# A graph network's setup in written order: first edges found eight at a time, one-hots from 16 bit operands, layer norm on ACT and POOL

## The chip, the cores and the metric

One core of a Trainium2 chip. The time is device time in microseconds, the median of several executions. Engines are named as in the profile: PE (matrix multiplications), DVE (vector operations), ACT (activations), POOL (which also issues the indirect transfers, that is gathers and scatters), SP (which here only issues plain transfers).

## The reference, cut to what matters

6250 nodes with 64 features, 206250 edges sorted by destination dst, so that the edges of a node lie together. Layer 0 and then three attention layers:

```python
h = relu(layernorm(x))
# layer 0: messages along edges, mean over the edges of a node
msg = relu(concat(h[dst], edge_attr_16) @ W1 + b1)
x = x + relu(segment_sum(msg, dst) / max(count, 1) + h @ Wres + bres)
h = relu(layernorm(x))
# three attention layers over the same edges, with edge_attr_32
for l in range(3):
    q, k, v, e = h @ Wq + bq, h @ Wk + bk, h @ Wv + bv, edge_attr_32 @ We
    a = softmax over the edges of a node of (q[dst] * (k[src] + e)) / sqrt(C)
    h = segment_sum(a * (v[src] + e)) + h @ Ws + bs      # and prelu after the first two
x = x + h
```

## The kernel before, in words

The nodes are padded to 6272 = 49 x 128 and sorted by their number of edges (degree). Block b holds the 128 nodes of about equal degree, one in each partition; its nodes get CAP[b] slots for edges (66 in block 0, 22 in block 48), of which LEAST[b] are surely filled.

**Setup** (gnn_kernel, lines 115 to 373, to 127 us). It finds where the edges of each node begin, counts degrees, sorts the nodes, and writes the table tabx with a row of 192 numbers for each node: -(h W1 + b1), h(W1 + Wres) + both biases, and x.
- *Coarse search.* dst is loaded twice, one shifted by one edge (prev, cur; 127 and 126), into space that belongs to k.rows. first (179) takes every 256th edge; pb (182) spreads it to all partitions through PE; count on DVE (191) or signs on ACT (196) count how many are below a node. From that run_i (204) picks, for each partition and each of 7 groups g of 7 nodes, where a window of 728 edges is gathered (got, 209).
- *Fine search.* For each of the 49 nodes of a partition and one more, a pass over the window counts the edges below it: 21 on ACT straight from the integers, 29 on DVE from a cast (look_f, 237).
- *Sort.* start, deg and the class cls come from that (249 to 269); oh (280) is a one-hot of the class, cnt, cum and at (282 to 297) give each node its place; half (304) splits it in column and row.
- *Permutation.* In seven rounds of seven nodes, one-hots to and blk and the products val = blk x of (312 to 319) are made on DVE, and PE multiplies them into pperm (321). join and what follows give at_i (first edge), num_i (number of the node), deg of each sorted node.
- *Rows of x* (334 to 370). In seven groups of seven blocks: sums, squares and root of the layer norm on DVE, POOL and ACT, transposes (361), relu to hT (364), projection with wn (367), copy to rx (368), x itself beside it (369), and write-back to tabx (370).
- src is turned (225 to 233) into edge order in DRAM (srcs).
- A check that dst does not fall (fall, 216) goes into bad; if any check fails, another path computes the result.

In this part the order of each engine's instructions is chosen by a scheduler that may interleave the sections above.

**Layer 0** (layer0, 443) is ordered by hand on POOL, PE, ACT and DVE: each engine runs its instructions as they stand in the code. For block b, POOL gathers edge attributes four blocks ahead (load_e, 457), rows of tabx (load_x, 463), src (load_src, 470) and edge_attr_32 six blocks back (load_ea). PE turns attributes (turn, 483), and messages (494) does PE products, DVE maxima and a tree of sums, 16 slots at a time; after each such chunk one entry of todo runs. finish(g) (538) closes a group of blocks (FIN0: 8, 8, 8, 8, 8, 4, 3, 2): it makes the new x, its sums, and on ACT the squares and root (562 to 565), and leaves the rest in todo: norm on DVE (568, 570), project, rows. put (594) scatters a row to the attention table, at most two in a block, LATE = 5 blocks after its group closed (626); the rest are put after the loop.

**Attention** (attention, 685), three layers: POOL gathers kv rows one slot of a block at a time (704, by way of 429), DVE does the arithmetic.

Of the kernel before, what the change touches and what calls it, by code (L numbers as in the profile page):

```python
# [25 lines left out]
F16 = mybir.dt.float16  # L26
AF = mybir.ActivationFunctionType
# [69 lines left out]
def gnn_kernel(ctx: ExitStack, tc: tile.TileContext, x, src_t, dst_t, dst_row, ea16, ea32, eaT16, eaT32, w, out):  # L97
# [17 lines left out]
    with tc.tile_pool(name="chk", bufs=1) as p, tc.tile_pool(name="chk2", bufs=2) as p2, \  # L115
            tc.tile_pool(name="n0w", bufs=2) as wp, tc.tile_pool(name="chkp", bufs=1, space=PSUM) as pp, \
            tc.tile_pool(name="n0p", bufs=2, space=PSUM) as psum:

# [6 lines left out]
        for r in (most, rest):  # L125
            nc.sync.dma_start(prev[r], by_row(dst_row[:EP])[r])
            nc.scalar.dma_start(cur[r], by_row(dst_row[1:])[r])
# [3 lines left out]
        sf = p.tile([P, T], I32, name="sf")  # L131
        nc.scalar.dma_start(sf, src_t)
        make_identity(nc, ident)
# [4 lines left out]

        nc.gpsimd.memset(k.w0blk, 0.0)
        for j in range(8):  # L140
            nc.sync.dma_start(k.w0blk[j * 16:(j + 1) * 16, j % 4 * D:(j % 4 + 1) * D], w["L0_gnn_W1"][D:, :])
        for l in range(LAYERS):
            for i, s in enumerate("qkvs"):
                nc.sync.dma_start(wl[l][:D, i * D:(i + 1) * D], w[f"L1_gnn_W{s}{l}"])
                nc.sync.dma_start(wl[l][D:D + 1, i * D:(i + 1) * D], w[f"L1_gnn_b{s}{l}"][None, :])
        nc.sync.dma_start(slope, w["L1_gnn_prelu_a"][None, :].to_broadcast([P, 1]))
        for l in range(LAYERS):
            nc.gpsimd.memset(k.wblk[l], 0.0)
            for j in range(4):
                nc.sync.dma_start(k.wblk[l][j * 32:(j + 1) * 32, j * D:(j + 1) * D], w[f"L1_gnn_We{l}"])  # L150
# [7 lines left out]

        node = iota(NB + 1, NB)
        nc.gpsimd.memset(ones, 1.0)  # L160
        iota(P, 0, f=col)
        place = iota(NB, 1, [[P, NB]])
# [4 lines left out]
        for t, values in ((k.cap, CAP), (least, LEAST)):  # L167
            for v, i, j in runs(values):
                nc.gpsimd.memset(t[:, i:j], float(v))
        going = p.tile([P, CLS, NB], BF16, name="going")  # L170
        nc.gpsimd.memset(going, 1.0)
        nc.gpsimd.memset(going[:, :, 0:1], 0.0)

        near = p.tile([P, NB + 1], F32, name="near")
        nc.vector.tensor_scalar(near, node, -0.5, None, op0=OP.add)
# [8 lines left out]
        less = p.tile([P, NB + 1], F32, name="less")  # L186
# [20 lines left out]
        for g in range(NG0):  # L207
            t = scratch[:, 2 * WE + g * LOOK:2 * WE + (g + 1) * LOOK]
            nc.gpsimd.indirect_dma_start(
                out=t, out_offset=None, in_=by_run,  # L210
                in_offset=bass.IndirectOffsetOnAxis(ap=run_i[:, g:g + 1], axis=0))
            got.append(t)

        nc.vector.memset(bad, 0.0)
        fall = p.tile([NW, WE], BF16, name="fall")
        nc.vector.tensor_tensor(fall, prev, cur, op=OP.is_gt)
        nc.vector.tensor_reduce(bad[:NW, 0:1], fall, axis=AX.X, op=OP.max)

        for t0 in range(0, T, 4 * P):
            n4 = min(4, -(-(T - t0) // P))  # L220
            ps = psum.tile([P, 4, P], F32, name="ps", tag="pr_t")
            si = wp.tile([P, 4, P], I32, name="si")
            sff = wp.tile([P, 4 * P], F32, name="sff")
            nt = min(4 * P, T - t0)
            nc.scalar.copy(sff[:, :nt], sf[:, t0:t0 + nt])
            for i in range(n4):
                n = min(P, T - t0 - i * P)
                nc.tensor.transpose(ps[:n, i, :], sff[:, i * P:i * P + n], ident)
            for i in range(n4):
                n = min(P, T - t0 - i * P)  # L230
                nc.scalar.copy(si[:n, i, :], ps[:n, i, :])
                e0 = (t0 + i * P) * P
                nc.scalar.dma_start(srcs[e0:e0 + n * P].rearrange("(t e) -> t e", e=P), si[:n, i, :])

        for g in range(NG0):
            f = p2.tile([P, LOOK], F32, name="look_f", bufs=3)
            (nc.gpsimd.tensor_copy if g else nc.scalar.copy)(f, got[g])
            for i in range(SG + (g == NG0 - 1)):
                b = SG * g + i
                if i < NA:  # L240
                    signs(got[g], b, less[:, b:b + 1], [P, LOOK], BF16)
                else:
                    count(f, b, less[:, b:b + 1], [P, LOOK], BF16)
        by_group = lambda t: t.rearrange("p (g i) -> p g i", i=SG)
        nc.vector.tensor_scalar(by_group(less[:, :NB])[:, :, :NA], by_group(less[:, :NB])[:, :, :NA], 0.5, LOOK / 2,
                                op0=OP.mult, op1=OP.add)
        start = p.tile([P, NB + 1], F32, name="start")
        nc.vector.tensor_scalar(run, run, float(RUN), -1.0, op0=OP.mult, op1=OP.add)
        nc.vector.tensor_add(by_group(start[:, :NB]), by_group(less[:, :NB]), run[:, :, None].to_broadcast([P, NG0, SG]))
        nc.vector.tensor_add(start[:, NB:], less[:, NB:], run[:, NG0 - 1:])  # L250
        nc.vector.tensor_scalar(start, start, 0.0, float(E), op0=OP.max, op1=OP.min)

        deg = p.tile([P, NB], F32, name="deg")
        nc.vector.tensor_sub(deg, start[:, 1:], start[:, :NB])
        nc.vector.tensor_scalar(deg, deg, 0.0, float(P - 1), op0=OP.max, op1=OP.min)
        whole = p.tile([P, 2, NB], I32, name="whole")
        nc.vector.tensor_copy(whole[:, 0], start[:, :NB])
# [4 lines left out]
        of = p.tile([P, NB, 4], F16, name="of")  # L262
        nc.vector.tensor_copy(of, part.rearrange("p v i b -> p b (v i)"))
        cls = p.tile([P, NB], F32, name="cls")
        nc.vector.tensor_scalar(cls, deg, float(LOW), float(HIGH[0]), op0=OP.max, op1=OP.min)
        for h in HIGH:
            nc.vector.scalar_tensor_tensor(cls, deg, float(h), cls, op0=OP.is_gt, op1=OP.add)
        nc.vector.scalar_tensor_tensor(cls, deg, 0.0, cls, op0=OP.is_gt, op1=OP.add)
        nc.vector.tensor_scalar(cls, cls, -float(LOW), float(CLS - 1), op0=OP.add, op1=OP.min)


        for l in range(LAYERS):
            nc.gpsimd.tensor_copy(k.ws[l][:, :D], wl[l][:, 3 * D:])
            nc.gpsimd.tensor_scalar(k.ws[l][:, D:2 * D], wl[l][:, :D], float(D // HEADS[l]) ** -0.5, 0.0, op0=OP.mult,
                                    op1=OP.add)
            nc.gpsimd.tensor_copy(k.ws[l][:, 2 * D:], wl[l][:, D:3 * D])


        oh = p.tile([P, CLS, NB], BF16, name="oh")
        nc.vector.tensor_tensor(oh, col[:, :CLS, None].to_broadcast([P, CLS, NB]),  # L280
                                cls[:, None, :].to_broadcast([P, CLS, NB]), op=OP.is_equal)
        cnt = p.tile([P, CLS], F32, name="cnt")
        nc.vector.tensor_reduce(cnt, oh, axis=AX.X, op=OP.add)
        pc = pp.tile([P, 2, CLS], F32, name="pc", tag="pc")
        nc.tensor.matmul(pc[:, 0, :], ones, cnt, start=True, stop=True)
        nc.tensor.matmul(pc[:, 1, :], before, cnt, start=True, stop=True)
# [7 lines left out]
        nc.vector.tensor_add(cum, cum, upto[:, :, None].to_broadcast([P, CLS, NB]))  # L294
        nc.vector.tensor_mul(cum, cum, oh)
# [7 lines left out]
        half = p.tile([P, 2, NB], F32, name="half")  # L303
        nc.vector.tensor_copy(half, half_i)
        turned = p.tile([P, NB], F32, name="turned")
# [3 lines left out]
        pperm = pp.tile([P, 4, NB], F32, name="pperm", tag="pc")  # L309
        for b0 in range(0, NB, 7):  # L310
            to = p2.tile([P, 7, P], F16, name="to")
            nc.vector.tensor_tensor(to, col[:, None, :].to_broadcast([P, 7, P]),
                                    half[:, 1, b0:b0 + 7, None].to_broadcast([P, 7, P]), op=OP.is_equal)
            blk = p2.tile([P, 7, NB], F16, name="blk")
            nc.vector.tensor_tensor(blk, col[:, None, :NB].to_broadcast([P, 7, NB]),
                                    half[:, 0, b0:b0 + 7, None].to_broadcast([P, 7, NB]), op=OP.is_equal)
            val = p2.tile([P, 7, 4, NB], F16, name="val")
            nc.vector.tensor_mul(val, blk[:, :, None, :].to_broadcast([P, 7, 4, NB]),
                                 of[:, b0:b0 + 7, :, None].to_broadcast([P, 7, 4, NB]))
# [123 lines left out]
def layer0(tc, ea16, ea32, ident, tabx, srcs, k, col, least, ones, bad, nbad_i):  # L443

    nc = tc.nc
    with tc.tile_pool(name="g0", bufs=3) as gp, tc.tile_pool(name="e0", bufs=2) as ep, \
# [152 lines left out]
        with tc.manual_schedule(engines={getattr(mybir.EngineType, e) for e in ("Pool", "PE", "Activation", "DVE")}):  # L599
# [25 lines left out]
            for b in range(NB):  # L625
# [13 lines left out]
                if b + 1 < NB:  # L639
                    turn(b + 1)  # L640
# [746 lines left out]
```

## Time and profile before

| | us |
|---|---|
| median of 8 runs (7579.67 to 7613.91) | 7593.4 |
| the profiled execution | 7585.84 |
| its span (first to last instruction) | 7584.1 |
| setup, to the first gather from tabx | 127.1 |
| layer 0, to the first gather of kv | 449.5 |
| attention | 7007.5 |

Engine totals over the span:

```profile
PE 1752.7 (23%) x4808; PEld 1105.4 (15%) x4808; DVE 3178.6 (42%) x6020; ACT 353.3 (5%) x1096; POOL 5057.7 (67%) x5212
```

How to read the lines that follow: a group's line has line, engine, operation, output<-input, shape and count, then busy time, mean ns of one, idle time just before it and what ended most of that. In the timeline the first number is the start, the second how long, and the bracket the idle time before and its releaser. In a table by stage the columns after the stage's length are busy us (and instructions) of each engine, the granted PE clock, the share of the transfer engines and GB/s. A line of waits has the total, the times and the longest.

### The profile page before, as it was taken

How to read it: one execution, taken by the hardware profiler on the slowest of the kernel's cores; microseconds unless marked ns; L12 is line 12 of the kernel's file. 1: busy time of each engine (PE TensorE's matmuls, PEld its weight loads, DVE VectorE, ACT ScalarE, POOL GpSimd, SP SyncE). 2: the span in 40 equal slices, each digit the busy share in tenths (PEclk: the TensorE clock that was granted, in tenths of full speed). 3: DMA queues.
4: the chain of work that ended last, by engine and by line, in shares of the span. 5: the costliest groups of instructions: out<-in, count | busy, mean ns of one | idle time of the engine just before them, and what ended most of it. 6: DMA issues, size and time to landing. Idle time of an engine off the chain costs nothing. (4 is left out here: it accounts for less than half of the span.)

```text
span 7584.1 us, 26893 instructions
## 1 busy us (share of the span) xinstructions
PE 1752.7 (23%) x4808; PEld 1105.4 (15%) x4808; DVE 3178.6 (42%) x6020; ACT 353.3 (5%) x1096; POOL 5057.7 (67%) x5212
## 2 busy tenths in 40 slices
PE   4652221122222222211221221222211111121111
PEld 3431111111111111100111111111111111111100
DVE  7873333353333444433443443445433333344333
ACT  2110000000000000000000000000000000000000
POOL 4566666666666665777666766765777777667775
PEclk8765555555555555555555555555555555555555
DMA  3653222222222222222222222221222222222221
GB/s 97 210 178 95 70 69 69 72 73 74 65 76 70 71 74 57 63 59 56 59 60 57 63 59 54 64 60 55 67 57 57 60 55 59 56 62 61 57 59 40
DMA packets 226262, 534.67 MB, mean 70 GB/s; under 512 B 89430, under 2 KB 105148, under 8 KB 224982
## 3 DMA queue, kind: packets, MB, share of 16 engines
q0 software_dynamic: 171200, 374.08, 19.3%
q1 hardware_dynamic: 52790, 156.27, 6.4%
q10 hardware_dynamic: 2090, 2.48, 0.1%
q14 instruction: 141, 1.16, 0.1%
q8 instruction: 41, 0.67, 0.0%
HBM read 458.63 MB, written 73.87 MB: 70 GB/s over the span
## 5 line engine op out<-in xcount | busy, mean ns | idle before, releaser
L429 POOL DMA_INDIRECT kv<-tab,src x4788 | 4697.5, 981 | 2152.4 <-issue 1549.8
L763 DVE TENSOR_TENSOR kv<-kv,pe 128x1024 f32<-128x1024 f32 (+6 forms) x663 | 737.7, 1113 | 3350.0 <-remote 2385.5
L757 PE MATMUL pe<-wblk,ea 128*128 128x256 f32 x1736 | 851.4, 644 | 2846.7 <-issue 1327.6
L757 PEld LDWEIGHTS pe<-wblk,ea 128*128 128x128 f32 x1736 | 504.5, 317 | 3166.0 <-issue 1798.3
L799 DVE TENSOR_REDUCE some<-kv 128x64 f32<-128x512 f32 (+6 forms) x690 | 611.1, 920 | 59.7 <-remote 36.4
L772 DVE TENSOR_TENSOR prod<-kv,more 128x512 f32<-128x512 f32 (+6 forms) x690 | 425.0, 627 | 152.0 <-remote 78.3
L773 DVE TENSOR_REDUCE al<-prod 128x16 f32<-128x512 f32 (+10 forms) x690 | 423.8, 626 | 104.6 <-remote 32.6
L757 PE MATMUL pe<-wblk,eaT 128*128 128x256 f32 x868 | 375.2, 588 | 300.7 <-DVE kv L763 155.7
L795 DVE TENSOR_TENSOR kv<-kv,more 128x512 f32<-128x512 f32 (+6 forms) x690 | 416.0, 625 | 0.0
L816 PE MATMUL po<-ws,ht 65*128 65x256 f32 x196 | 114.2, 686 | 1073.3 <-issue 903.9
L734 PE MATMUL turn<-ident,ea 128*128 128x128 f32 x434 | 113.8, 400 | 1013.9 <-issue 780.9
L757 PEld LDWEIGHTS pe<-wblk,eaT 128*128 128x128 f32 x868 | 249.8, 306 | 378.0 <-DVE kv L763 170.6
L734 PEld LDWEIGHTS turn<-ident,ea 128*128 128x128 f32 x434 | 70.6, 198 | 1071.8 <-issue 834.8
L816 PEld LDWEIGHTS po<-ws,ht 65*128 65x128 f32 x196 | 53.1, 313 | 1119.5 <-issue 936.2
L506 PE MATMUL pm<-w0blk,eT 64*128 64x256 f32 x868 | 177.6, 530 | 107.5 <-DVE msg L509 70.5
L429 POOL DMA_INDIRECT e<-in_ea_dram,at_i x98 | 104.5, 1067 | 127.2 <-PE turn L491 87.6
L784 ACT ACTIVATE more<-al,m 128x33 f32<-128x33 f32 (+22 forms) x245 | 72.0, 294 | 2024.4 <-issue 1058.5
L531 DVE TENSOR_TENSOR msg<-msg 128x128 f32<-128x128 f32 (+12 forms) x221 | 136.4, 617 | 7.2
L788 DVE TENSOR_REDUCE s<-more 128x2 f32<-128x66 f32 (+34 forms) x147 | 30.9, 210 | 258.5 <-ACT more L784 213.5
L506 PEld LDWEIGHTS pm<-w0blk,eT 64*128 64x128 f32 x868 | 111.5, 256 | 156.6 <-issue 76.9
L435 POOL DMA_INDIRECT out_dram<-hn,num_i x49 | 53.3, 1088 | 99.8 <-DVE hn L820 43.0
L735 ACT COPY eaT<-turn 128x512 f32<-128x512 f32 (+3 forms) x127 | 66.5, 524 | 1140.2 <-remote 813.6
(194 smaller groups left out, 1458.9 us busy)
## 6 DMA issues: line engine op xcount, KB each, us to landing
kv<-tab,src POOLq DMA_INDIRECT x4788
ea<-eat SPq DMA_DIRECT2D x26, 576.0 KB
ea<-eat SPq DMA_DIRECT2D x24, 512.0 KB
ea<-eat SPq DMA_DIRECT2D x16, 640.0 KB
ean<-e SPq DMA_DIRECT2D x13, 576.0 KB
ea<-ean SPq DMA_DIRECT2D x13, 576.0 KB
eat<-eaT SPq DMA_DIRECT2D x13, 576.0 KB
ea<-eat SPq DMA_DIRECT2D x16, 448.0 KB
```

What stands on the lines that cost most here:

```text
L429: return nc.gpsimd.indirect_dma_start(out=out, out_offset=None, in_=table, in_offset=bass.IndirectOffsetOnAxis(ap=idx, axis=0))
L506: nc.tensor.matmul(pm[:, r, u].rearrange("p j f -> p (j f)"), eT[h, t0 // 8 + u, :], k.w0blk[h, :], start=True, stop=True)
L531: nc.vector.tensor_add(msg[:, :h] if c > 2 else total, msg[:, :h], msg[:, c - h:c])
L734: nc.tensor.transpose(ps[:, i - i0, :], t[:, i, :], ident)
L757: nc.tensor.matmul(pe[:, 4 * g:4 * g + 4].rearrange("p j f -> p (j f)"), ea[:, t0 // 4 + g, :], k.wblk[l], start=True, stop=True)
L763: nc.vector.tensor_add(pair(kv[:, :m, :2 * D]), pair(kv[:, :m, :2 * D]), pe[:, :m, None, :].to_broadcast([P, m, 2, D]))
L772: nc.vector.tensor_mul(prod[:, :n], kv[:, :n, :D], q[:, None, :].to_broadcast([P, n, D]))
L773: nc.vector.tensor_reduce(al[:, :H, t0:t0 + n].rearrange("p h j -> p j h"), prod[:, :n].rearrange("p j (h c) -> p j h c", h=H), axis=AX.X, ...
L784: nc.scalar.activation(ex[:, h, :c], al[:, h, :c], AF.Exp, bias=m[:, h:h + 1])
L795: nc.vector.tensor_mul(v.rearrange("p j (h c) -> p j h c", h=H), v.rearrange("p j (h c) -> p j h c", h=H), ex[:, :H, t0:t0 + n].rearrange( ...
L799: nc.vector.tensor_reduce(some[:, i, :], v.rearrange("p j f -> p f j"), axis=AX.X, op=OP.add)
L816: nc.tensor.matmul(po, ht[:, :P], k.ws[l + 1], start=True, stop=True)
```

## The change

All of the setup now also runs in written order, on all five engines. What it does, section by section:
- SP alone issues the transfers: prev, x, the weights of layer 0, src; later the attention weights, x straight into the last third of tabx, cur, slope, We.
- Windows are cast to f32 on ACT into looks, with the group's eight nodes appended (LOOK8 = 736 elements), and one max_index per group gives the index of the first match of eight nodes. The indices are made monotone by a scan from the end. Only the last border keeps a sign pass.
- The layer norm's squares go to ACT, one block at a time between the casts; the norm itself to ACT (even quads of blocks) and POOL (odd ones).
- One-hots have the node as the innermost dimension, with col spread to 16 bit (colb); cls, half and of are 16 bit too. Two rounds (24 and 25 nodes) instead of seven. PE reads their slices [:, :, b].
- Rows of x go by quads of four blocks, q 0 to 3 before the first round's products, 4 to 6 before the second's, the rest after.
- src is turned last.
- Layer 0: the fall check comes before the first block's messages; the place column of k.rows is filled at block 3; the squares become an entry of todo, with an empty one behind; LATE is 6.

```diff
+    with tc.manual_schedule(engines={... "Pool", "PE", "Activation", "DVE", "SP"}), \
...
+        colb = [k.src[i].bitcast(F16)[:, :D * NB].rearrange("p (c b) -> p c b", b=NB) for i in range(2)]
+        nc.vector.tensor_copy(colb[0], col[:, :D, None].to_broadcast([P, D, NB]))
+        nc.scalar.copy(colb[1], col[:, D:, None].to_broadcast([P, D, NB]))
...
+        def squares(b):
+            sq = p2.tile([P, D], F32, name="sq0")
+            nc.scalar.activation(sq, xs[:, b], AF.Square, bias=negm[:, b:b + 1], accum_out=var[:, b:b + 1])
...
         for g in range(NG0):
+            nc.scalar.copy(looks[:, g, :LOOK], got[g])
+            nc.vector.max_index(place_i[:, g], node[:, SG * g:SG * g + 8], looks[:, g])
+            for b in range(2 * g, 2 * g + 2):
+                squares(b)
+        signs(got[NG0 - 1], NB, less, [P, LOOK], BF16)
+        for b in range(2 * NG0, NB):
+            squares(b)
+        nc.scalar.activation(var, var, AF.Sqrt, bias=eps[:, 0:1], scale=1.0 / D)
...
+        nc.sync.dma_start(tabx[:, 2 * D:], x)
+        for r in (most, rest):
+            nc.sync.dma_start(cur[r], by_row(dst_row[1:])[r])
...
+        nc.vector.tensor_tensor_scan(from_[:, ::-1], start[:, ::-1], start[:, ::-1], float(E), op0=OP.min, op1=OP.min)
...
+        nc.vector.reciprocal(var, var)
+        nc.vector.tensor_mul(negr, negm, var)
...
+        def norm(q):
+            for b in quads[q]:
+                if q % 2:
+                    nc.gpsimd.tensor_scalar(hn[:, b], xs[:, b], var[:, b:b + 1], negr[:, b:b + 1],
+                                            op0=OP.mult, op1=OP.add)
+                else:
+                    nc.scalar.activation(hn[:, b], xs[:, b], AF.Identity, bias=negr[:, b:b + 1], scale=var[:, b:b + 1])
...
+        def rows_of_x(q):
+            if q < len(quads):
+                norm(q)
+            if 1 <= q <= len(quads):
+                turn(q - 1)
+            if 2 <= q:
+                project(q - 2)
...
+        parts = [slice(0, 24), slice(24, NB)]
+        for i, s in enumerate(parts):
+            n = s.stop - s.start
+            for c in range(2):
+                nc.vector.tensor_tensor(to[:, c * D:(c + 1) * D, s], colb[c][:, :, s], half[:, 1:2, s].to_broadcast([P, D, n]),
+                                        op=OP.is_equal)
+            nc.vector.tensor_tensor(blk[:, :, s], colb[0][:, :NB, s], half[:, 0:1, s].to_broadcast([P, NB, n]),
+                                    op=OP.is_equal)
+            for v in range(4):
+                nc.vector.tensor_mul(val[:, v, :, s], blk[:, :, s], of[:, v:v + 1, s].to_broadcast([P, NB, n]))
+            for q in ((0, 1, 2, 3), (4, 5, 6))[i]:
+                rows_of_x(q)
+            for b in range(s.start, s.stop):
+                nc.tensor.matmul(pperm.rearrange("p v b -> p (v b)"), to[:, :, b],
+                                 val[:, :, :, b].rearrange("p v c -> p (v c)"), start=(b == 0), stop=(b == NB - 1))
...
+        for q in range(7, len(quads) + 2):
+            rows_of_x(q)
...
-            for i in range(n):
-                sq = wp.tile([P, D], F32, name="sq")
-                nc.scalar.activation(sq, x[:, i], AF.Square, bias=m[:, i:i + 1], accum_out=v[:, i:i + 1])
-            nc.scalar.activation(v[:, :n], v[:, :n], AF.Sqrt, bias=eps[:, 0:1], scale=1.0 / D)
+            def squares():
...
-            todo = [norm]
+            todo = [squares, lambda: None, norm]
...
-        AHEAD, LATE, LATER = 4, 5, 6
+        AHEAD, LATE, LATER = 4, 6, 6
...
+            nc.vector.tensor_tensor(fall, scratch[:NW, WE:2 * WE], scratch[:NW, :WE], op=OP.is_gt)
+            nc.vector.tensor_reduce(bad[:NW, 0:1], fall, axis=AX.X, op=OP.max)
...
+                if b == 3:
+                    nc.gpsimd.iota(k.place, pattern=[[P, NB]], base=0, channel_multiplier=1)
+                    nc.gpsimd.tensor_copy(k.rows[:, :, 4 * D:4 * D + 1], k.place[:, :, None])
+                    nc.gpsimd.memset(k.rows[:, :, 4 * D + 1:], 0.0)
```

turn(q) transposes a quad of hn through PE and writes its relu to k.ht on ACT; project(q) multiplies it with wn, copies on ACT and writes 128 of the 192 columns of tabx.

## The prediction

> **What bounds the kernel now.** I read the page first. POOL's row is the highest and one line makes it:
>
> ```profile
> span 7584.1 us, 26893 instructions
> ...
> L429 POOL DMA_INDIRECT kv<-tab,src x4788 | 4697.5, 981 | 2152.4 <-issue 1549.8
> ```
>
> That line is the three attention layers. Then I cut the span at the places where the work changes hands; the columns are busy time by engine, granted PE clock, DMA share and GB/s.
>
> ```profile
> 0.00:28.10 28.10, 6.79 (x28) 5.77 (x28) 14.02 (x32) 8.25 (x20) 10.63 (x76) 1.00 0.60 163
> 28.10:60.10 32.00, 0.43 (x1) 0.14 (x1) 26.04 (x58) 22.38 (x52) 13.66 (x23) 1.00 0.33 105
> 60.10:85.70 25.60, 20.61 (x88) 17.46 (x88) 24.13 (x46) 10.71 (x22) 14.42 (x19) 1.00 0.20 81
> 85.70:112.40 26.70, 13.52 (x72) 10.80 (x72) 24.63 (x31) 3.50 (x7) 6.73 (x8) 0.76 0.13 52
> 112.40:127.10 14.70, 9.66 (x42) 8.12 (x40) 1.06 (x8) 4.38 (x9) 3.78 (x6) 0.50 0.35 122
> 127.10:576.60 449.50, 265.07 (x1247) 174.55 (x1247) 334.11 (x691) 78.91 (x272) 257.68 (x244) 0.70 0.57 180
> 576.60:7584.10 7007.50, 1436.60 (x3332) 888.53 (x3332) 2754.61 (x5157) 225.19 (x714) 4750.85 (x4837) 0.53 0.24 63
> ```
>
> The reader is to see that the change touches only the first 576.6 us; the 7007.5 us after them are not edited and move as a block. What counts is when that block starts. The setup is 127.1 us and a chain; the timeline gives its links:
>
> ```profile
> 13.10 0.17 DVE L179 CAST first<-rows 101x8 f32<-101x8 int32 x1 [10.96 <-DMA rows<-in_dst_row_dram]
> ...
> 28.16 1.19 POOL L209 DMA_INDIRECT rows<-in_dst_row_dram,run_i  x1 [2.59 <-DVE run L248]
> ...
> 60.12 0.16 DVE L250 TENSOR_TENSOR start<-less,run 128x1 f32<-128x1 f32 x1
> ...
> 111.39 0.36 DVE L324 COPY join<-pperm 128x196 f32<-128x196 f32 x1 [0.83 <-PE pperm L321]
> ...
> 127.10 0.95 POOL L429 DMA_INDIRECT rx<-tabx,num_i  x1 [3.45 <-DMA tabx<-rx]
> ```
>
> From 28 to 112 us DVE is 75 us busy of 84: it is the setup's limit, and from 112 PE is. Layer 0 (127 to 577) has DVE busy three quarters of the time, and POOL waits there for buffers, not buffers for POOL:
>
> ```profile
> POOL e L429 <- PE turn L491: 87.6, 20, 11.9
> ...
> DVE v L568 <- ACT v L565: 10.3, 7, 2.0
> ```
>
> So an earlier start of layer 0 should arrive at its end.
>
> **The change, part by part.** Rows used (mean ns of one after the bar's first number):
>
> ```profile
> L191 DVE TENSOR_SCALAR_CACHE_REDUCE lt<-look_f,iota 128x728 bf16<-128x728 f32 x29 | 26.0, 966 | 6.0 <-issue 6.0
> L196 ACT ACTIVATE sg<-rows,near 128x728 bf16<-128x728 int32 x21 | 18.6, 888 | 2.3 <-issue 2.3
> L361 PE MATMUL pr_t<-ident,hn 128*64 128x128 f32 x49 | 11.9, 421 | 36.1 <-POOL hn L356 36.1
> L367 PE MATMUL pr_o<-wn,hT 65*128 65x128 f32 x98 | 23.7, 433 | 0.9 <-ACT hT L364 0.6
> L318 DVE TENSOR_TENSOR val<-blk,of 128x1372 f16<-128x1372 f16 x7 | 11.8, 1689 | 0.0
> ```
>
> *Up to the gathers.* Today prev and cur (808 KB each) load together; from 2 to 10 us the stages show 225 to 270 GB/s, and first starts 3.6 us after the 1.6 MB would be through (2.0 + 7.5). With cur behind the weights on SP, prev is alone: 808 KB at 230 to 420 GB/s (both rates stand in stages before 18 us) is 2 to 3.5 us, so first starts near 8.0; ends 6.9 and 13.1 (no gain). SP's queue gets sf ahead of w0blk, and later tabx<-x, cur, slope; nothing before the gathers waits for those. The new copies of col (3136 elements, some 3.3 us on DVE and on ACT at the rate of L318 and L196) fit into the wait for prev. Then pb 4.0 us as now (13.10 to 17.1), to 12.0; four counts of 0.98 to 15.9 (today DVE and ACT do the fall check, sums of x and sff casts first); four small operations, 0.9 with POOL's wake: gathers from 16.8 instead of 28.16, **-11.4**.
>
> *Finding the edges.* Removed: 29 passes of L191 and 21 of L196, 32 us on two engines side by side. Added: 7 casts to f32 on ACT (0.80 each, the one at L237), 7 find instructions of 736 elements on DVE, one sign pass. The trace has no find. Its ends: the fixed 0.16 of a tiny operation, and eight passes of L191, 8 x 1.05 = 8.4 us; nearest is one pass (same engine, same length): 1.05. ACT also does two squares between casts: the layer 0 squares L564 start 0.33 apart, so 0.80 + 0.66 = 1.46 each. The first gather lands 1.19 + 3.15 after its start (28.16 to 32.50), at 21.1; gathers issue 1.25 apart and the last lands 4.5 after its issue, at 30.1; ACT reaches its end at 30.9; two squares and the sign pass to 32.6. So start is computed from 32.6 instead of 60.1: **-27.5** so far. POOL's wblk memsets, sff cast, cap and least lie beside this.
>
> The Trainium skill (Vector Engine (DVE) Microarchitecture Reference, section 3.9) describes FIND_INDEX_8 as comparing the stream with eight values at once, which would be one pass; no run here shows it yet.
>
> *From start to the one-hots.* The same operations by their own rows, without the layer norm between them: 1.0 (start, scan), 0.4, 1.0 (cls), 1.85 oh, 1.83 cnt, 1.27 (whole, part, of), 3.67 scan, 0.5, 2.13, 0.4 (reciprocal, negr), 1.85, 2.96, 1.5 = 20.4 us, to 53.0 (today first blk at 85.75). A wait is added: the reciprocal of var stands behind 49 squares on ACT; 35 are left after the sign pass, 35 x 0.33 = 11.6, plus table load and root 1.6: ready at 45.8. DVE comes there at 46.8. If the squares ran 0.52 apart (activation plus accumulator read in turn) DVE would wait 6 us, with all the rest of the permutation behind it.
>
> *One-hots and PE.* To, blk and val keep their 18,277 elements in 14 instructions for 21. At L318's 1.15 ns (most of the seven take 1.58 us), which is two 16 bit operands already, that is 10.4 + 10.8 us; the ends are this and nothing. I take this row, as it is the only one of its kind, though L318 repeats single elements and the new layouts don't. PE now runs in written order: q 1 to 3 of the x rows before part 0 (done by 56), 24 matmuls from 63.4 (7 take 1.30 at L321, 0.186 each) to 67.9, q 4 to 6 (a quad is 4 transposes of 0.243 and 4 projections of 0.479 = 2.9 us, from 7 in 1.70 and 14 records in 3.35, the same at clock 1.00 and 0.50) to 76.6, 25 matmuls to 81.3, then 25 transposes and 29 projections, 20.0, to 101.3. ACT needs 2.4 per quad at most, POOL's norms 1.0, both under PE's 2.9. Copy and write-back as today (122.87 to 127.10), 4.5: first rx gather at 105.8 instead of 127.1, **-21.3**. Of the 27.5, PE takes 6 back. The row order no longer hides x rows under DVE's passes; that is the new bound.
>
> A rule speaks on the one-hots: the same page, section 5.1, has two-source operations with 16 bit operands at two elements a cycle unless one element is repeated, which fits L318's one (1.58 us for 1372). By it the parts cost 5.9 and 6.1 us, and the gather would come at 101.3.
>
> *x into tabx* goes from DRAM directly, 6272 pieces of 256 B, issued after wl (about 34). Queue q10's 2090 packets up to 200 us took 4.4% of 16 engines, 0.067 us each; q0's over the whole run 0.137. That is 26 to 54 us, done by 88: hidden; it is late only if a piece takes over 0.18.
>
> A rule speaks against this edit: DMA: Bandwidth & Descriptors, section Specifications, wants at least 512 B for full rate. It gives no price that reaches 0.18 us, and the sum stays.
>
> *Layer 0.* The fall check (2.29 + 2.29) now stands before the first message on DVE. Today DVE starts layer 0 only when the last tabx write lands (eps waits 12.4 for it) and needs 8.4 us, while PE's first pm makes the message wait to 9.9 after the rx gather; with 4.6 more it is 13.0: **+3**, or -4 if DVE can start at 82 where its inputs are ready. Squares moved into todo: the seven waits of 2.0 go, **-8** (0 to -10.3; PE's next result can be what is late instead). LATE 6: nine rows instead of seven are put after the loop, but one pick fewer stands behind the last wait (6.71 at 563.49): **-1.3** (2.6 either way). POOL's place at b 3 is 0.7 us beside waits. The 10.0 us gap of DVE at 148.2 with no releaser I leave as it is; it could go or come elsewhere.
>
> Sum: -21.3 + 3 - 8 - 1.3 = -27.6. The profiled execution took 7585.84 (span 7584.1); so 7558.2. It lies 7.6 under the median 7593.4, so the median becomes **7566**.
>
> **Rivals.**
> - *PE is slow on the new layouts.* Weights and moving data of the 49 matmuls are read at a step of 98 B; no PE row has a step. DVE's strided reduce L297 takes 2.96 where L283 takes 1.83. On PE at three times 0.186, 18 us more: 7584. For: all of it is on PE's path. Against: DVE's factor is 1.6, which is 5 us.
> - *Layer 0 swallows the start.* If its transfers set its pace (DMA share 0.57; msg waits 27.2 for them), the end stays: 7593. Against: POOL's 87.6 us above.
> - *The find is no single pass* (slower). Place: DVE between gathers and start. At 8.4 each, 58.8 from 21.9, start is at 80.7, 48 later than forecast: 7614. The gain is gone from 6.3 us each. Against: nothing in the trace says that DVE reads data eight times; for: nothing shows the opposite.
> - *More is gained*: gap, eps and one-hots all go well: 10 + 7 + 4.5 more, 7544.
>
> **How the numbers follow.** Forecast 0.64 (7550 to 7578), more gained 0.06, PE slow 0.12, swallowed 0.08, find slow 0.07, another loss 0.03. What can be told from no change is 0.2%, 15 us: faster 0.70, same 0.20, slower 0.10. The range takes in forecast, PE slow and most of the larger gain: 7540 to 7585.
>
> **What would show it.** Right: first rows<-in_dst_row gather near 17, start near 33, to from 53, join near 81, rx gather near 106, kv gathers about 28 us earlier than 576.6. Wrong: a find over 2 us; val far from 1.4 us per 1176 elements; PE idle in the x rows (then a latency, not its work, sets the pace); v waiting for ACT still; kv's start not earlier; or a stage after it that is not 7007.5 us long. By the skill's rule val would take near 0.8 us.

## The result, and the profile after

The changed kernel takes 7554.57 us (median of 11 runs, 7531.52 to 7565.9), the one before 7595.09 beside it (32 runs). The ratio is 0.9944, 95% interval 0.9934 to 0.9954: faster by 35 to 50 us where 27.6 were forecast. The profiled execution took 7562.57.

The page of the changed kernel; the line of the attention's gathers has the same count as before and a little more time:

```profile
span 7560.9 us, 26851 instructions
...
L466 POOL DMA_INDIRECT kv<-tab,src x4788 | 4703.6, 982 | 2154.4 <-issue 1527.1
```

The stages, cut at the start of part 0 on PE, the join, the first rx gather and the first kv gather (busy us of PE, PEld, DVE, ACT and POOL, then PE clock, share of the transfer engines, GB/s):

```profile
63.90:92.50 28.60, 28.60 (x87) 14.62 (x87) 5.81 (x7) 4.75 (x10) 9.87 (x18) 1.00 0.09 28
92.50:120.33 27.83, 22.01 (x103) 20.42 (x102) 2.81 (x14) 12.97 (x29) 1.02 (x1) 1.00 0.43 120
120.33:546.77 426.44, 267.33 (x1242) 176.40 (x1240) 337.51 (x690) 79.34 (x272) 262.28 (x248) 0.72 0.60 189
546.77:7560.90 7014.13, 1430.78 (x3332) 884.78 (x3332) 2751.43 (x5157) 224.76 (x714) 4756.79 (x4837) 0.53 0.24 63
```

The timeline, at the links that the prediction showed of before (start, length, and in the bracket the idle time and what ended it):

```profile
8.01 0.47 DVE L182 CAST first<-rows 101x8 f32<-101x8 int32 x1 [4.37 <-DMA rows<-in_dst_row_dram]
...
15.25 1.06 DVE L194 TENSOR_SCALAR_CACHE_REDUCE lt<-pb,iota 128x808 bf16<-128x808 f32 x1 [6.78 <-ACT sg L199]
...
20.25 1.14 POOL L212 DMA_INDIRECT rows<-in_dst_row_dram,run_i  x1 [11.80 <-DVE run L216]
...
25.34 0.92 DVE L230 FIND_INDEX8 place_i<-iota,raw 128x8 uint32<-128x736 f32 x1
...
63.90 10.32 PE L379 MATMUL pperm<-raw,to 128*128 128x196 f16 x24 [4.35 <-DVE raw L375]
...
92.52 0.36 DVE L382 COPY join<-pperm 128x196 f32<-128x196 f32 x1 [22.77 <-PE pperm L379]
...
119.70 0.06 DVE L487 MEMSET eps<- 128x1 f32 x1 [8.25 <-DMA srcs<-si]
...
120.33 0.95 POOL L466 DMA_INDIRECT rx<-tabx,num_i  x1 [5.47 <-DMA srcs<-si]
```

Before, all 49 matmuls of pperm took 8.5 us of PE; now the first 24 alone take 10.3:

```profile
L321 PE MATMUL pperm<-val,to 128*128 128x196 f16 x49 | 8.5, 348 | 9.6 <-DVE val L318 9.6
```

The size is about right, and that is luck, since its two parts miss in opposite directions. The setup gives 6.8 us in place of 21.3: DVE is idle for 22.77 us ahead of the join, PE is busy without a break from 63.9 to 110, and what releases layer 0 is no longer tabx but srcs. Layer 0's stage gives 23.1 us (449.5 to 426.4) in place of 6.3. The two profiled executions lie only 23.3 us apart (7585.84 and 7562.57), since the first is 9 us under its median and the second 8 over.

### The profile page after: what moved, and what is told of

Same layout as the page of the kernel before. It is cut to its first block, busy times and chain, and to the rows that moved or that the text cites. A ratio compares the mean times of both kernels' runs of the same rounds, so it can differ in the third digit from the quotient of the medians.

```text
span 7560.9 us, 26851 instructions
## 1 busy us (share of the span) xinstructions
PE 1760.7 (23%) x4808; PEld 1105.9 (15%) x4808; DVE 3140.0 (42%) x5942; ACT 359.8 (5%) x1158; POOL 5060.5 (67%) x5203
```

## Experiments

Each run is compared with runs of the kernel before on its own chip, and the chips differ: on some, before takes 7591 to 7614 us, on two others 6630 to 6639. The traces of the first kind have waits of up to 11 us on DVE in layer 0 that end with a release for which the trace names no engine ("remote"). They sum to 32 to 51 us a profile and lie mostly at other places from run to run; the traces of the second kind have none of them there. So stages are compared within a kind, and a stage of the first kind, read from one profile, is uncertain by some of that sum.

| kernel | before there | first rx | first kv | between | ratio (95%) |
|---|---|---|---|---|---|
| before | | 127.1 | 576.6 | 449.5 | |
| changed | 7595 | 120.3 | 546.8 | 426.4 | 0.9944 (0.9934-0.9954) |
| e3 layer 0 edits alone | 7614 | 127.2 | 562.4 | 435.2 | 0.9970 (0.9957-0.9984) |
| e4 changed, without them | 7614 | 117.8 | 567.2 | 449.4 | 0.9978 (0.9966-0.9989) |
| e5 before, 60 more on DVE | 7614 | 127.7 | 584.7 | 457.0 | 1.0004 (0.9993-1.0016) |
| e1 sources early | 7614 | 114.4 | 533.8 | 419.4 | 0.9951 (0.9934-0.9968) |
| e15 changed, LATE 5 | 7591 | 120.3 | 549.6 | 429.3 | 0.9957 (0.9942-0.9972) |
| e12 before, 13 more on PE | 6630 | 127.0 | 518.5 | 391.5 | 1.0000 (0.9990-1.0010) |
| e11 changed, dense matmuls | 6630 | 121.6 | 497.4 | 375.8 | 0.9968 (0.9956-0.9979) |
| e8 changed, counts apart | 6639 | 120.6 | 496.1 | 375.5 | 0.9963 (0.9949-0.9977) |
| e7 node outermost | 6639 | 156.7 | 531.5 | 374.8 | 1.0018 (1.0008-1.0027) |
| e2 sources, checks | 6639 | 112.5 | 484.4 | 371.9 | 0.9950 (0.9934-0.9967) |
| e10 and values side by side | 6630 | 93.4 | 464.5 | 371.1 | 0.9922 (0.9909-0.9936) |

The theory after the result: PE's stepped operands and srcs ate the setup's gain, and the layer 0 edits carry the stage. Rivals: the stage gained because the 10.0 us gap went, and the setup lost to something else (the clock, the counts).

**e3 and e4: layer 0's edits alone, and the change without them.**

```diff
-            todo = [norm]
+            todo = [squares, lambda: None, norm]
...
-        AHEAD, LATE, LATER = 4, 5, 6
+        AHEAD, LATE, LATER = 4, 6, 6
```

> The kernel before with the layer 0 edits alone (squares into the list of work between messages, LATE 6); setup unchanged. Theory: of the 23 us by which layer 0's stage became shorter, the waits of v for ACT (10.3 us in 7 waits before, 1.5 after) and the last wait for ends (6.7 before, 3.6 after) belong to these edits, so the first kv gather moves from 576.6 to 563-566 and the time falls by 10 to 13 us; the 10.0 us gap before the second message at 148.2 stays. Rival: the edits only move waits about, and the whole 23 us is the gap and the earlier setup; then the first kv gather stands at 574-577 and the time within 3 us of before.

> The changed kernel with the layer 0 edits undone (squares at the end of each group, LATE 5); its setup stays. Theory: v waits for ACT again (8 to 10 us in seven waits), the first kv gather moves from 546.8 to 556-560, and the time is 10 to 13 us above the changed kernel's. Rival (the edits do nothing by themselves): first kv gather at 546-549.

The edits alone bring the first kv gather to 562.4 (14.2 earlier), with the gap still there (149.97, after 10.77 idle). Without them the stage is 449.4, as long as before's, though there the gap is gone. So the edits carry the stage and the gap's going does not show in it; e4's kv gather (567.2) came later than either theory said. An estimate supports this over all profiles of the first kind: take from each stage DVE's waits that end with "remote" or "issue" (46 us before, 45 in e4, 50 in e5; 44 in the changed kernel, 53 in e3, 35 in e1, 44 in e15). Left are 404, 405 and 407 us with before's order of layer 0, and 382, 382, 385 and 386 with the changed one.

e4's setup has the same instructions as the changed kernel's and still ends 2.5 us sooner, though its part 0 starts 1.8 us later (65.70). The trace shows why: the eight projections of a quad take 1.92 us at 100.06 and 1.10 us at 102.62, so PE's clock opened in between (recorded at 102.7), which it didn't do there in the changed kernel.

**e5 and e12: does the gap follow the count of instructions?**

```diff
+        for _ in range(60):
+            nc.vector.memset(dull, 0.0)        # e5, at the start
+        for _ in range(13):
+            nc.tensor.matmul(dull, ident, ident[:, :8], start=True, stop=True)   # e12, behind pb
```

> The kernel before with 60 one-element memsets on DVE ahead of its first work, in time that DVE idles until 13.1 us (60 x some 0.06 us). Theory (the 10.0 us gap at 148.2, DVE's 245th recorded instruction, is code not yet loaded, counted in instructions): the gap moves 60 instructions back in the program, to near the 185th of before, which lies ahead of layer 0 in time where DVE waits anyway; the second message follows the first at once and the first kv gather moves from 576.6 to 566-568. Rival 1 (the gap belongs to the place: the second message waits for something that the trace doesn't name): gap of 10 us still ahead of the second message, first kv gather within 2 us of 576.6. Rival 2 (the gap moves but lands where it costs as much, among the 41 tests of full): first message 10 us later, first kv gather unchanged.

> The kernel before with 13 more small fp32 matmuls on the PE behind pb (24 to 30 us, PE idle). Theory: the 10.0 us gap ahead of the second message is the PE's (its signal for the second group of matmuls comes late because its next code is not there), counted in the PE's instructions; 26 instructions and their loads earlier it falls where the PE waits for e anyway, the second message follows the first within 1 us, and the first kv gather moves from 576.6 to about 568. Rival 1: the gap belongs to the place, as it did when DVE's instructions were shifted: 8 to 11 us ahead of the second message. Rival 2: it belongs to the chip; on a chip that shows no such waits in layer 0 neither place nor count will show it.

The timeline of e5 at the first two messages, then that of e12:

```profile
137.71 1.23 DVE L512 TENSOR_TENSOR msg<-pm,rx 128x1024 f32<-128x1024 f32 x1 [3.50 <-PE pm L509]
146.91 1.23 DVE L512 TENSOR_TENSOR msg<-pm,rx 128x1024 f32<-128x1024 f32 x1 [7.97 <-remote]
```

```profile
135.85 2.35 DVE L512 TENSOR_TENSOR msg<-pm,rx 128x1024 f32<-128x1024 f32 x2 [1.94 <-PE pm L509]
```

Sixty more instructions on DVE left the gap where it was, ahead of the second message (7.97 us), so the theory that counts DVE's instructions falls. In this profile the kv gather even came 8.1 us later, with the medians the same. e12 has no gap, but it ran on a chip whose traces have no such waits at all, so it doesn't tell PE's count from the chip. What makes these waits stays open.

**e1 and e2: the sources early, then the checks in the setup too.** e1 moves the block that turns src ahead of the one-hots (with four buffers for si); e2 also moves fall ahead of join, and no, over, full and lack behind k.num.

> The changed kernel with the turning of the source numbers put ahead of the one-hots (ACT after the root, PE idle there, SP's stores ahead of those of tabx). Theory: the start of layer 0 waits for the last of these stores (eps 8.2 us, the first gather of rx 5.5 us), so without them the first rx gather moves from 120.3 to 113-114, when the last rows of tabx have landed, the first message from 131.0 to 124-125, and the first kv gather from 546.8 to 539-541; the time falls by 6 to 7 us. Rival: layer 0 is bound by its gathers or by tabx's stores, so that the first rx gather is not earlier than 118, or the stage behind it swallows what it gains: first kv gather at 545-548.

> The sources early (as in the run before) and the check for falling numbers, no, over, full and lack moved from the head of layer 0 into the setup, where DVE waits for the PE (69.8 to 92.5 us and 93.9 to 110 us). Theory: the 11.3 us of these on DVE stand between the landing of the first rows and the first message, so the first message moves from 125.1 (sources early) to 118-120 (e turned at 119 to 121.5, first rx gather at 114.4 and 3 us to land), the first kv gather from 533.8 to about 528, the time 6 us under that of sources early. Rival 1: the first message waits for its rows anyway, and moves by under 3 us. Rival 2: the stage is bound by its gathers on POOL (1.25 us each), and the first kv gather stays within 3 us of 533.8.

```profile
114.42 0.95 POOL L466 DMA_INDIRECT rx<-tabx,num_i  x1 [1.68 <-DMA tabx<-rx]
```

e1: the first rx gather comes at 114.4, released by tabx; the first message at 125.07 in place of 130.98; kv 13 us earlier (more than the 6 of its start; the waits of those two kinds in its stage sum to 9.5 us less). The wait for srcs is shown, and its price is 6 us. e2: the first message stands 8.9 us behind the rx gather in place of 10.65, and waits 9.46 us for PE's pm: rival 1, the rows and PE were next in line. On one chip e2 has its kv gather 11.7 us ahead of e8 (the changed kernel with the counts apart), 8.1 of it from the start. Some 2 of these 8.1 us belong to neither edit: in e2 PE's clock was open from 78.4 to 85.2 (recorded), and the two quads there took less.

**e6: what the step costs.** Behind the join, four groups of 24 matmuls; kind 0 both operands with the step, 1 weights side by side, 2 values side by side, 3 both.

```diff
+                wt = flat_to[:, b * P:(b + 1) * P] if kind & 1 else to[:, :, b]
+                mv = flat_val[:, b * 196:(b + 1) * 196] if kind & 2 else val[:, :, :, b].rearrange("p v c -> p (v c)")
+                nc.tensor.matmul(probe, wt, mv, start=(b == 0), stop=(b == 23))
```

> The changed kernel with four groups of 24 more matmuls of 128x196 f16 behind the join, all into a PSUM tile that nobody reads: operands as in the change (both with a step of 98 bytes), weights side by side and values with the step, weights with the step and values side by side, both side by side. Theory: the step makes the difference between 0.186 us (before) and 0.43 us (after), so the first group takes 0.43 each and the last 0.19. If the weight load is what pays, the second group is at 0.19 and the third at 0.43; if the moving values pay, the other way round; if each pays a part, both lie between. Rival: the layouts are innocent and the clock, or the reading of val while DVE works, is what made them slow: all four groups the same. The first rx gather comes later by the groups' sum, 22 to 42 us.

These instructions alone (length, PE busy, clock column), the last stretch inside kind 3:

```profile
93.22:103.37 10.15, 10.14 (x24) 1.00 0.00 0
103.38:113.48 10.10, 10.10 (x25) 1.00 0.00 0
113.49:117.40 3.91, 3.91 (x25) 1.00 0.02 4
118.50:119.97 1.47, 1.47 (x19) 1.00 0.00 0
```

Kinds 0 and 1: 0.42 us each; kind 2: 0.16. The whole price is the moving values'; the weights' step costs nothing that shows. At 118.4, 5 us into the dense matmuls, the pace doubles within kind 3 (0.16 to 0.08), and a quad of x rows then takes 1.34 us where it took 2.56 at 75 us. The clock column reads 1.00 throughout: up to the first recorded transition (here 118.5) it says nothing, and only the durations show that PE had been at half pace.

**e11: PE's clock opened by dense matmuls.**

```diff
+                nc.tensor.matmul(warm, full_f16[:, :P], full_f16[:, P:P + 512], start=True, stop=True)   # x16 behind pc, x20 ahead of part 0
```

> The changed kernel with dense f16 matmuls of 512 columns into a PSUM tile that nobody reads: 16 behind pc (44 to 52 us, PE idle) and 20 ahead of part 0 (59.5 to 64, PE idle). Theory: the PE ran at half its speed through the whole setup, though busy without a gap from 63.9 to 110 us, since matmuls with a step and fp32 ones do not open its clock and dense ones do (the rows of x took 2.56 us a quad in the changed kernel and 1.34 behind 5 us of dense matmuls); opened at 48, the quads take 1.34 us (ACT then sets 1.9). If the stepped values run by the PE's clock too (0.21 us each), the join moves from 92.5 to 79-81 and the first rx gather from 120.3 to 103-106; if the stepped read has a pace of its own (0.42 us), the join moves to 88-89 and the first rx gather to 110-112, should the clock stay open. Rival: the clock closes again behind the first stepped matmuls or never opens; join at 92 or later, first rx gather 120 to 124.

Its stages: dense matmuls, part 0, the quads behind it, and the rows of x at the end:

```profile
59.60:65.00 5.40, 5.40 (x22) 2.27 (x20) 5.37 (x7) 1.92 (x5) 5.40 (x4) 0.80 0.20 59
65.00:75.30 10.30, 10.30 (x26) 3.69 (x25) 5.24 (x7) 0.00 (x0) 8.92 (x17) 0.67 0.01 2
75.30:82.80 7.50, 7.50 (x37) 7.08 (x36) 0.00 (x0) 4.05 (x9) 0.00 (x0) 0.50 0.22 65
93.60:111.00 17.40, 17.40 (x84) 16.55 (x82) 1.26 (x7) 10.06 (x23) 0.00 (x0) 0.50 0.28 84
```

The clock opens on the dense matmuls (0.22 us for 512 columns, from 0.43), at 48.1 and, after it had closed at 55.0, again at 61.8. It closes at 68.6, inside part 0, where the stepped matmuls take 0.42 us at either clock; it stays at 0.50 through 36 us in which PE is busy all the time. So the rival holds: join at 93.6, rx at 121.6. The step has a pace of its own, and the clock closed under it, as it did in e2 (at 85.2, in part 1). The theory that fp32 matmuls do not open the clock is too strong: it opened during the rows of x in e2 and e4.

**e7: DVE writes the layout that PE likes.**

```diff
-        to = p.tile([P, P, NB], F16, name="to")
+        to = p.tile([P, NB, P], F16, name="to").rearrange("p b c -> p c b")     # val likewise
```

> The changed kernel with to and val stored node outermost, as the PE likes them; DVE makes them from the same 16 bit operands in the same order, but writes with a step of 256 or 392 bytes. Theory: pperm's matmuls go back to 0.19 us (4.6 and 4.7 us for the two parts instead of 10.3 and 10.8), and DVE keeps its two elements a cycle since its inputs are as they were: one-hots 11.6 us, join at 81 instead of 92.5, first rx gather at 109 instead of 120.3, time -11 us. Rival 1: the stepped write halves DVE's rate, one-hots 22 us, part 1 ready at 80, join at 86, first rx gather at 114. Rival 2: the stepped write is slower still (4 us and more for one half of to); the join is then no earlier than 92.

Its timeline on DVE:

```profile
58.54 13.89 DVE L370 TENSOR_TENSOR to<-src,half 128x1536 f16<-128x1536 f16 x2
...
73.08 20.81 DVE L375 TENSOR_TENSOR raw<-blk,of 128x1176 f16<-128x1176 f16 x4
```

PE's parts fall to 3.57 and 4.09 us, but a stepped write costs DVE 5.2 us per 1176 elements in place of 0.81: rival 2, slower than before the change.

**e8: the counts apart.** ACT's sums go into run_a, DVE's stay in run.

> The changed kernel with ACT's three sums of signs in a tile of their own and DVE's four counts in run. Theory: DVE waited for ACT (6.78 us idle ahead of its first count, which begins at 15.25 right after ACT's last) because both wrote columns of one tile; apart they run side by side from 12.4, the first gather moves from 20.25 to about 17, start from 37.25 to 34, the first rx gather from 120.3 to 117, the time by -3 us. Rival 1: the wait is for the PSUM tile that both read, and nothing moves. Rival 2: they do run side by side but slow each other down (each pass 1.06 to nearly 2 us), and the gather comes at 19 to 20 all the same.

DVE still waits 6.78 us, until ACT's last sum; the first gather is at 19.80. So it isn't the tile of the sums. What both still share is the PSUM tile pb (rival 1); two copies of it were not tried, so the cause is argued and not shown.

**e10: the values side by side, in the order in which DVE writes them.** On top of e2:

```diff
-            nc.vector.tensor_tensor(blk[:, :, s], colb[0][:, :NB, s], half[:, 0:1, s]...
-            for v in range(4):
-                nc.vector.tensor_mul(val[:, v, :, s], blk[:, :, s], of[:, v:v + 1, s]...
+            nc.vector.tensor_tensor(blk[:, s], col[:, None, :NB]..., half[:, 0, s, None]..., op=OP.is_equal)
+            nc.vector.tensor_mul(val[:, s], blk[:, s, None, :]..., of.rearrange("p v b -> p b v")[:, s, :, None]...)
```

> Sources early and checks in the setup as before, and val and blk made node outermost, in the order of their bytes (DVE at one element a cycle for these two), while to stays as the change has it. Theory from the four groups of matmuls measured apart: the step costs the moving values alone (0.42 us against 0.16), the weights' step nothing. So pperm's parts take 4 us each in place of 10.3 and 10.8; DVE takes 8.2 and 8.4 us for its two parts in place of 5.7 and 6.0; part 0 starts at 66.5 in place of 64 and the join comes at 82 to 84 in place of 92.5; the first rx gather, 112.5 with sources early and checks in the setup, comes at 101 to 104, and the time is 8 to 10 us under that kernel's, some 0.6 per cent under before. If the PE's clock opens on the dense matmuls, the rows of x run at 1.34 us a quad in place of 2.56 and it comes at 95 to 98. Rival: DVE's slower passes eat it (part 1 ready after 88), and the join stays at 90 or later.

PE's two parts and the rows of x between them in e10:

```profile
66.96 4.08 PE L391 MATMUL pperm<-raw,to 128*128 128x196 f16 x24 [6.33 <-DVE raw L386]
...
72.29 0.60 PE L340 MATMUL pr_t<-ident,hn 128*64 128x128 f32 x4
...
75.65 2.30 PE L391 MATMUL pperm<-raw,to 128*128 128x196 f16 x25 [0.53 <-DVE raw L386]
```

Part 0 takes 4.1 us at 0.16 a matmul. The clock opens at its end (recorded at 71.1, open for 20.5 us); a quad's transposes then take 0.60 us in place of 1.06, and part 1 takes 2.3 us in place of 10.8. The join comes at 80.0 and the rx gather at 93.4, 19.1 us ahead of e2. The ratio of 0.9922 makes it the fastest kernel here: 51 us under before, where the change with dense matmuls (e11) has 21 on the same chip.

**e15: LATE back at 5.**

> The changed kernel with LATE back at 5; the squares stay in the list of work. Measured so far from the first rx gather to the first kv gather, on chips whose trace has no stops of unnamed origin in layer 0: 391.5 us with before's layer 0, 375.5 and 375.8 with the change's; on chips with such stops 449.5 and 426.4. Theory: the squares and the empty place behind them are the whole of it (the PE's transposes of a group wait 63.3 us for DVE's h before and 13.6 after, v for ACT 12.3 and 2.0), LATE nothing but the last puts: the stage is 375 to 379 us (426 to 434 with stops), the time within 4 us of the changed kernel's. Rival: LATE carries half of it (a put and an ends that ACT or POOL no longer waits for), the stage is 383 us or more (438 or more), the time 8 us higher.

The stage is 429.3 us, 2.9 over the change's; on chips of this kind one order of layer 0 has given stages further apart than that (449.5 before, 457.0 in e5). LATE has no price that these runs resolve; the squares carry the stage.

The waits behind that, over layer 0, first before's order (e12), then the change's (e8):

```profile
PE pt L578 <- DVE h L573: 63.3, 8, 9.2
...
DVE v L571 <- ACT v L568: 12.3, 8, 2.0
```

```profile
PE pt L615 <- DVE h L610: 13.6, 5, 3.6
...
DVE v L608 <- ACT v L605: 2.0, 3, 1.2
```

## Why the prediction was right or wrong

| step | forecast | measured |
|---|---|---|
| first | 8.0 | 8.01 |
| gathers | -11.4 | -7.9 (28.16 to 20.25) |
| finding edges | 1.05 us a find, start at 32.6 | 1.0 us (0.09 + 0.92), start at 37.25 |
| start to one-hots | 20.4 us | 20.9 us (58.12) |
| one-hots | 10.4 + 10.8 | 5.7 + 6.0 |
| pperm | 0.186 each: 4.5 + 4.7 | 0.42 each: 10.1 + 10.6 |
| quads 4 to 6, tail | 8.7 + 20.0 | 7.7 + 17.9 |
| tail to the rx gather | 4.5 | 10.1 |
| first rx gather | 105.8 | 120.33 |
| layer 0 | +3 - 8 - 1.3 | -23.1 (chips without the waits: -16) |

- *Up to the gathers* failed by 3.5 us: the sum had DVE's four counts from the end of pb, and they wait for ACT's three signs. Before shows the same order (ACT's three sums from 19.38 to 22.23, DVE's first count at 22.39), which the sum overlooked.
- *Finding the edges* held to 1.2 us (17.0 from the first gather to start, 15.8 forecast; the last window came 7.4 us after its issue, 4.5 forecast). The rival of a find that is no single pass falls with FIND_INDEX8 at 0.92 us. Two slips around this changed nothing: by the sum's own terms the last window lands at 29.1 and not 30.1 (ACT's chain ends at 30.7 all the same), and the gain would be gone from a find of 5.5 us and not 6.3.
- *The one-hots* failed to the good. I took L318's row, which repeats single elements. The estimate by the Trainium skill's rule (Vector Engine (DVE) Microarchitecture Reference, section 5.1) was 5.9 and 6.1 us, and the trace agrees with it: 5.7 and 6.0, with val at 0.81 us per 1176 elements. This cancelled 4.6 of the 5.1 us that part 0's operands were late.
- *PE* is the term that was mis-sized: 0.186 us had no step in it. The rival that PE is slow on the new layouts was right by its mechanism, with a factor of 2.3 where three was priced: 11.5 us. Its reason was half right, since only the moving operand pays. The sum also took PE's prices to be the same at clock 1.00 and 0.50. They are not: a quad takes 2.56 us at half pace and 1.34 at the open clock (e6), and before's groups of seven matmuls take 1.30 us, but the one at 98.77 takes 0.76. The 1.00 of the early stages was the column ahead of its first transition.
- *Copy and write-back as today* failed: the prediction took tabx as what layer 0 waits for, and did not price src, which now stands last. That is 5.6 us; e1 takes it away.
- Of the 14.5 us missing at the rx gather, part 0's later start makes 0.5, pperm 11.5, the wait for srcs 5.6; the quads and the tail give 3.1 back.
- *Layer 0*: of the squares I priced only the wait of v. PE's transposes of the group stand in order behind that chain, and the next block's products behind them: PE's wait for h falls from 63.3 to 13.6 us, DVE's waits for pm from 18.2 to 10.3, beside v's from 12.3 to 2.0. Together the last two give 18.2 us on DVE; less 1.8 for a later first message (10.65 against 8.9 behind the rx gather; forecast +3) it comes near the 16.0 us that the stage loses on the chips without unnamed waits (391.5 in e12, which stands for before there, to 375.5). No run there has the layer 0 edits alone; that they carry the stage is shown by e3 and e4.
- *The gap* that was left as it is went away, but e4 shows no gain from it. It stood ahead of the second message in all three profiles of the first kind with before's setup (before, e3, e5) and in none with the changed one; why is open. That the stage lost 23.1 in one pair of profiles against 16 elsewhere lies within what the unnamed waits vary.
- The attention is 7014.1 long for 7007.5, one execution each. On the quieter chips e11's kv gather is 21.1 us earlier than e12's and its median 21.4 less than before's: what the stages ahead gain arrives at the end. On the others the medians differ by more than the profiles' kv gathers (40.5 against 29.9 us for the change, 25 against 14 for e3, 22 against 9 for e4); that is not resolved.

## What to carry to other kernels

Before a layout is changed for one engine, ask what the step does to the engine that reads it, which operand pays, and whether it can be written in order for both: here 1.1 ns an element on DVE in place of 0.69 (5.1 us for 3.0) bought 6.2 and 8.5 us on PE, the second with the clock open. When a chain is moved out of the way, price everything that stands in order behind it, on every engine. When a section is put last, ask what waits for its last store: the first gather of rx waited for srcs, which it doesn't read (presumably its buffers take over memory of that section; no run separates this).

## What the runs showed of the hardware

- A moving operand of 128x196 f16 with a step of 98 bytes takes PE 0.42 us (e6), at either clock (e11); side by side it takes 0.16 us at half pace and 0.085 at the open clock (e6, e10). Weights with that step cost nothing that shows (0.16 with and without, e6).
- PE busy without a break is not PE at its full clock. The Trainium skill (TensorE: Matmul & The Clock Gate, Part 1) has the clock open after a busy window of some 3.4 us. Dense f16 matmuls did that within 2 to 5 us (e6, e10, e11). In the changed kernel stepped matmuls and the rows of x kept PE busy for 46 us (63.9 to 110) and its quads stayed at 2.56 us, the half pace. An open clock closed 3.6 and 4.7 us into stepped matmuls (e11, e2).
- The rows of x, fp32 matmuls without a step, did not open the clock in 18 us in the changed kernel, but it opened during them in e2 (at 78.4, 3.5 us into them) and in e4 (at 102.7, 8.6 us into them), with the same matmuls. What decides it is open, and it moves the first rx gather by 2 to 4 us from run to run.
- A stepped f16 write costs DVE 4.4 ns an element (e7, 5.20 us for 1176) against 0.69 in order.
